# Perceiver kernel: the last share of x added on TensorE, normalising on ScalarE, values by token tile, and context loops with more lag and halved accumulations

## The chip, the cores and the metric

The kernel runs on one core of a Trainium2 chip. The metric is the device time of one execution in microseconds. The kernel before took 1700.06 us (median of three runs, 1695.6 to 1703.4). The engines are called by the profile's names: PE (TensorE; PEld is its weight load), DVE (VectorE), ACT (ScalarE), POOL (GpSimd) and SP (SyncE, which here issues most loads).

## What is computed

Two layers of a perceiver, all in float32. x is 512 tokens by 512 features, the context 8192 by 512; there are 16 heads of 32. Each of six steps adds to x a function of its layer norm (without weights):

```python
x = x + L0_xattn(_layernorm(x), ctx, ...)        # 512 queries against the keys the mask leaves
x = x + L0_attn(_layernorm(x), ...)              # self attention, keys j >= i
x = x + L0_ffn(_layernorm(x), ...)               # 8 experts, top 2, x * sigmoid(x)
x = x + L1_xattn(_layernorm(x), ctx, ctx, ...)   # cross attention with another mask
x = x + L1_attn(_layernorm(x), ...)              # self attention in a window of 64
x = x + L1_ffn(_layernorm(x), ...)               # 8 experts, top 2, relu squared
```

In the first cross attention the queries and keys are normalised per head, with weights. Of the context's 64 tiles of 128 keys the masks leave few; the kernel lists the tiles that have a key left and works on 15 such tiles ("slots"). A slower path for longer lists is in the program and isn't taken with these inputs.

## The kernel before

x stays in SBUF as four token tiles of 128 x 512. The 16 heads are worked on as four groups (g = 0 to 3) of four heads (h), so that one group fills 128 partitions: four matmuls with 32 rows or 32 columns of the array each. Scores are held keys by queries, 128 x 512 for one head and one slot. The softmax's maximum of each query is found first (`maxima`), and is then taken off the scores inside PSUM by a small bf16 matmul (`subtract`, L644) of three rows, the maximum split in three bf16 parts (`shift`), so that ACT's exp needs only the key's mask as its bias.

**Order.** Every engine works through its own queue in program order, and waits on semaphores that the framework places from the tiles' use. A tile pool hands out buffers; `bufs` is how many of one tag there are, and a tile waits until the earlier one in its buffer is read out. A pool that is opened in space that a closed pool left waits for that pool.

**Stages**, with their place in the profiled span: the list of context tiles (0 to 20 us), layer norm and queries (to 79), keys of layer 0's cross attention with the maxima of group 0 (to 201), its attention loop (to 476), outputs and layer norm (to 493), self attention 0 (to 641), router (to 672), experts (to 930), end and a branch for overfull experts (to 948), keys of layer 1's cross attention (to 1110), its attention loop (to 1353), outputs and layer norm (to 1372), self attention 1 (to 1480), router (to 1505), experts (to 1677), end (to 1698.5).

**The keys' loop** (`attend_slots`, first half). For slot s: `keys(s)` projects on PE into `pk` and adds a bias on DVE into `kb` (two buffers, L1055); `settle(s - 1)` transposes the unit keys of the slot before (`ktp`, L1064); `maxima(0, s - 2)` computes scores of group 0 and takes the maximum on DVE (L770); then perhaps one `values`; then `unit(s)`, the normalisation of `kb` on ACT and DVE (L1105, L1109). In layer 0 ACT also scans layer 1's mask (L1210) in this stage. In layer 1 `settle` is empty.

**The attention loop** (L876 and on), 60 turns (four groups, 15 slots). A turn computes scores of group g, slot i, and in the first 41 turns also those for the maxima of 19 turns later. It does so in two batches (j = 0, 1) of two heads each: two `sc`, two `scm` (three buffers), two subtractions, two exp on ACT (L874), two maxima on DVE (L770). After the batch j = 0 comes `accumulate` (L829): the four matmuls of the turn before, exp(scores) times values, 512 columns each, into one PSUM bank `acc`. POOL sums the exponentials of four slots (`add_up`, L847), and `denominators` (L856) sums those over the keys on PE with a matrix of ones into `den`, which has one of the four buffers of the scores ("s"). `divide` (L866, DVE) makes the reciprocals from PSUM in halves, and POOL multiplies. Such extra steps ("fillers": the transposes `mtp` and `stp` of the next shift, `denominators`, `divide`, `outputs`, and in layer 0 six steps that list layer 1's tiles) are queued with the turn in which they are due, one in a turn. In the last turns, without maxima, all four heads go in one batch.

**Outputs** (L717, L720): the group's normalised result times Wo on PE into `ops`, which DVE adds to x, group by group. The last group is finished in halves (`finish_part`: copy on ACT L697, reciprocal L687, product L688, bias L691 on DVE).

**Layer norm** (L187 to L198), per token tile: bn_stats and bn_aggr on DVE, square root on ACT, reciprocal and normalising on DVE (`xn`, L194), four transposes on PE (`lnt`, L197), copy on ACT (L198).

**Self attentions** follow an order written out by hand, a string for `in_order`: q and k are projections (`prj`, L1258), V the values of one token tile, M maxima, S shift, W weighted sums, F finish, O outputs, E and T the last group's parts. Their weights are loaded on SP's queue when the stage's pool opens.

**The FFN's end** (L1879 to L1886): DVE adds the rows gathered for each token (`got` times its gate) to x; a last matmul (`xps`, L1883) adds the rows of the tail, and DVE adds that to x. A branch on overfull experts (L1889 to L1892) follows, whose body isn't executed here.

Of the kernel before, what the change touches and what calls it, by code (L numbers as in the profile page):

```python
# [57 lines left out]
def tile_perceiver(  # L58
# [6 lines left out]

    const = ctx.enter_context(tc.tile_pool(name="const", bufs=1))
# [9 lines left out]
    dram = ctx.enter_context(tc.tile_pool(name="dram", bufs=1, space=bass.MemoryType.DRAM))  # L76
# [22 lines left out]
    with tc.tile_pool(name="begins", bufs=1) as tmp, tc.tile_pool(name="beginsps", bufs=1, space=PSUM) as tps:  # L99
# [60 lines left out]

    def bcast(pool, name, n):

        t = pool.tile([P, n], F32, name=f"bc_{name}", tag=f"bc_{name}", bufs=1)
        nc.sync.dma_start(out=t, in_=a[name].partition_broadcast(P))
        return t
# [16 lines left out]
    def layernorm_t(pool, psum, tag, xnT, off, order=range(NT), after=None):  # L182

        xn = pool.tile([P, NT, D], F32, name="xn", tag="xn", bufs=1)
        for t in order:
            st = small.tile([P, 6], F32, name="ln_s", tag="ln_s")
            nc.vector.bn_stats(st, x[:, t, :])  # L187
# [6 lines left out]
            nc.vector.tensor_scalar(xn[:, t, :], x[:, t, :], mv[:, 0:1], r, ALU.subtract, ALU.mult)  # L194
# [3 lines left out]
            nc.scalar.copy(xnT[:, :, off + t * P : off + (t + 1) * P], tp)  # L198
            if after is not None:
                after(t, xn)  # L200
        return xn

# [219 lines left out]
    def cross_attention0():  # L422
        with ExitStack() as st:
            pool = st.enter_context(tc.tile_pool(name="c0", bufs=2))
            ctxp = st.enter_context(tc.tile_pool(name="ctxp0", bufs=2))
            psum = st.enter_context(tc.tile_pool(name="c0ps", bufs=2, space=PSUM))
            pacc = st.enter_context(tc.tile_pool(name="c0acc", bufs=1, space=PSUM))
# [3 lines left out]
            with tc.tile_pool(name="c0q", bufs=2) as qp:  # L431
# [8 lines left out]
            kvp = st.enter_context(tc.tile_pool(name="c0kv", bufs=NCHUNK // 2))  # L440
# [70 lines left out]
    def cross_attention1():  # L511
        with ExitStack() as st:
            pool = st.enter_context(tc.tile_pool(name="c1", bufs=2))
            ctxp = st.enter_context(tc.tile_pool(name="ctxp1", bufs=2))
            psum = st.enter_context(tc.tile_pool(name="c1ps", bufs=2, space=PSUM))
            pacc = st.enter_context(tc.tile_pool(name="c1acc", bufs=1, space=PSUM))
# [3 lines left out]
            with tc.tile_pool(name="c1q", bufs=2) as qp:  # L520
# [7 lines left out]
            kvp = st.enter_context(tc.tile_pool(name="c1kv", bufs=NCHUNK))  # L528
            mp = st.enter_context(tc.tile_pool(name="c1m", bufs=2))
# [38 lines left out]
    def tile_list(tmp, psum, counts, bad, tag, out):  # L568
# [8 lines left out]
        nc.tensor.transpose(tp, counts, ident)  # L577
        nc.vector.tensor_copy(rows, tp)
# [4 lines left out]
        nc.tensor.matmul(ps, lhsT=tri, rhs=some, start=True, stop=True)  # L583
        place = tmp.tile([n, 1], F32, name="place", tag="place")
# [7 lines left out]
        nc.tensor.matmul(ps[:, SLOTS : SLOTS + 1], lhsT=ones[0:n, 0:1], rhs=some, start=True, stop=True)  # L592
        row = tmp.tile([1, SLOTS + 1], F32, name="row", tag="row")
# [10 lines left out]
        ps = psum.tile([P, SLOTS], F32, name="kbp", tag=tag)  # L604
        nc.tensor.matmul(ps, lhsT=rows, rhs=taken, start=True, stop=True)
        kbias = small.tile([P, SLOTS], F32, name="kbias", tag="kbias")
        nc.vector.tensor_scalar(kbias, ps, 1.0, BIG, ALU.subtract, ALU.mult)
# [22 lines left out]
    def in_quads(pool, psum, pacc, qT, wo, bv, late, splits=None):  # L630
# [55 lines left out]
        def divided(g, r, d, den):  # L686
            nc.vector.reciprocal(d[:, r], den)  # L687
            nc.vector.tensor_tensor(k.o[g][:, r], k.o[g][:, r], d[:, r], ALU.mult)  # L688
            if bv is not None:

                nc.vector.tensor_scalar(k.o[g][:, r], k.o[g][:, r], bv[:, g : g + 1], None, ALU.add)  # L691
# [21 lines left out]
        def outputs(g, tiles):  # L713

            for t in tiles:
                ps = tile_s(name="ops")
                nc.tensor.matmul(  # L717
                    ps, lhsT=k.o[g][:, t * P : (t + 1) * P], rhs=wo()[:, g, :], start=True, stop=True
                )
                nc.vector.tensor_tensor(x[:, t, :], x[:, t, :], ps, ALU.add)  # L720
# [1435 lines left out]
```

## Time and profile before

The profiled execution took 1700.19 us, its span is 1698.5 us; 1.7 us lie around the span. TensorE's granted clock is 0.938 of full on average.

| stage, us | PE busy | DVE busy | ACT busy | POOL busy | granted clock |
|---|---|---|---|---|---|
| 20 to 79, queries | 50.98 of 59 | 31.18 | 17.18 | 15.81 | 0.94 |
| 79 to 201, keys of layer 0 | 109.81 of 122 | 73.53 | 70.50 | 8.50 | 0.96 |
| 201 to 476, attention loop 0 | 268.89 of 275 | 182.08 | 153.70 | 164.92 | 0.96 |
| 476 to 493, outputs, layer norm | 7.86 of 17 | 12.72 | 3.12 | 1.48 | 0.84 |
| 493 to 641, self attention 0 | 137.91 of 148 | 71.99 | 38.34 | 16.29 | 0.91 |
| 672 to 930, experts 0 | 254.95 of 258 | 37.20 | 38.33 | 19.08 | 0.99 |
| 1110 to 1353, attention loop 1 | 239.55 of 243 | 155.19 | 147.12 | 163.82 | 0.99 |
| 1353 to 1372, outputs, layer norm | 10.59 of 19 | 12.81 | 3.44 | 0.96 | 0.72 |
| 1372 to 1480, self attention 1 | 94.14 of 108 | 62.44 | 25.00 | 6.65 | 0.94 |
| 1677 to 1698.5, end | 8.13 of 21.5 | 8.22 | 0.82 | 0.00 | 0.58 |

A row is one stretch of the span, with the busy time of each engine in it and the share of the full clock that PE was granted. A busy PE may still be slow: a matmul that lasts longer at a lower clock, or whose neighbour waits for a buffer, counts as busy. In the profile's other lines `out<-in` are the names of tiles, `128*32` the weights and `128x512` the moving operand of a matmul, and `[2.87 <-DVE o L691]` the idle time ahead of an instruction and what ended it. One float32 matmul makes two records, so an accumulation of four matmuls shows as x8.

### The profile page before, as it was taken

What the parts mean: (1) busy time and instruction counts of PE and PEld (TensorE: products, weight loads), DVE (VectorE), ACT (ScalarE), POOL (GpSimd) and SP (SyncE); (2) the same over time, 40 slices, a digit from 0 to 9 for tenths busy, and PEclk for the clock granted to TensorE, in tenths of its full rate; (3) what the DMA queues carried; (4) which work ended last, traced back from release to release, by engine and by line L of the source; (5) the groups of instructions that cost most, each with busy time, mean ns of one, the idle gap of its engine ahead of it and who ended that gap; (6) DMA issues with size and microseconds to landing.
All of it is one profiled execution on the core that took longest, in us unless ns stands there. A gap on an engine that the chain in (4) does not pass through costs nothing. (4 is left out here: it accounts for less than half of the span.)

```text
span 1698.5 us, 24206 instructions
## 1 busy us (share of the span) xinstructions
PE 1559.3 (92%) x9877; PEld 908.3 (53%) x9877; DVE 775.3 (46%) x1394; ACT 570.7 (34%) x1081; POOL 446.5 (26%) x345
## 2 busy tenths in 40 slices
PE   5888999999979996999999799999999989779996
PEld 2333333333234446999998456433333245369995
DVE  5466677774633655111112133667765526831112
ACT  1356355556622231111111211155556612211110
POOL 6000057787110011000002100078786010010002
PEclk9999989999989977999999899899999989879996
DMA  7145200000030004877784400000000040066572
GB/s 249 50 136 180 74 1 1 1 1 1 1 131 1 1 1 177 326 257 267 284 293 155 156 26 19 25 1 1 1 1 1 1 152 11 25 237 216 187 246 92
DMA packets 83928, 169.32 MB, mean 100 GB/s; under 512 B 5106, under 2 KB 20498, under 8 KB 82384
## 3 DMA queue, kind: packets, MB, share of 16 engines
q1 hardware_dynamic: 77200, 147.87, 25.4%
q0 software_dynamic: 6016, 17.55, 3.0%
q10 hardware_dynamic: 576, 2.10, 0.4%
q8 instruction: 84, 1.38, 0.3%
q14 instruction: 52, 0.43, 0.1%
HBM read 156.82 MB, written 9.63 MB: 98 GB/s over the span
## 5 line engine op out<-in xcount | busy, mean ns | idle before, releaser
L874 ACT ACTIVATE pT<-sc,kbias 128x512 f32<-128x512 f32 x480 | 299.4, 687 | 205.3 <-PE sc L644 142.8
L757 PE MATMUL sc<-qTf,kTf 32*128 32x512 f32 x1264 | 299.4, 660 | 6.1 <-DVE d L866 4.9
L770 DVE SCALAR_TENSOR_TENSOR mx<-scm,kbias,mx 128x512 f32<-128x512 f32 x312 | 215.4, 743 | 98.2 <-PE scm L757 95.8
L757 PE MATMUL scm<-qTf,kTf 32*128 32x512 f32 x656 | 241.2, 654 | 2.1 <-DVE mx L770 2.1
L1801 PE MATMUL y<-hT,w 128*128 128x112 f32 (+13 forms) x1536 | 211.0, 297 | 0.6 <-DVE hT L1976 0.6
L1785 PE MATMUL hps<-tokens,w 128*128 128x112 f32 (+13 forms) x1536 | 208.5, 295 | 0.0
L1801 PEld LDWEIGHTS y<-hT,w 128*128 128x128 f32 x1536 | 204.3, 197 | 2.5 <-DVE hT L1976 0.8
L1785 PEld LDWEIGHTS hps<-tokens,w 128*128 128x128 f32 x1536 | 201.5, 195 | 1.7
L847 POOL TENSOR_TENSOR four<-four,pT 128x2048 f32<-128x2048 f32 x42 | 190.7, 4540 | 9.7 <-ACT pT L874 6.7
L757 PEld LDWEIGHTS sc<-qTf,kTf 32*128 32x128 f32 x1264 | 91.3, 190 | 147.8 <-issue 111.5
L847 POOL TENSOR_TENSOR four<-pT 128x2048 f32<-128x2048 f32 x24 | 109.0, 4544 | 109.2 <-ACT pT L874 109.2
L829 PE MATMUL acc<-pT,vNf 128*32 128x512 f32 x960 | 133.7, 623 | 1.5 <-ACT o L836 1.5
L770 DVE SCALAR_TENSOR_TENSOR mx<-sc,kbias,mx 128x512 f32<-128x512 f32 x136 | 93.3, 744 | 80.3 <-PE sc L757 80.3
L1976 DVE TENSOR_TENSOR hT<-sg,hps 128x264 f32<-128x264 f32 (+7 forms) x64 | 28.0, 437 | 189.5 <-ACT sg L1975 189.5
L644 PE MATMUL sc<-shift,ones 3*128 3x512 bf16 (+3 forms) x544 | 100.1, 383 | 3.6 <-DVE shift L679 3.6
L757 PEld LDWEIGHTS scm<-qTf,kTf 32*128 32x128 f32 x656 | 75.0, 188 | 49.8 <-DVE mx L770 38.0
L1826 POOL DMA_DIRECT2D answers_d<-yb x17 | 9.5, 559 | 311.5 <-ACT yb L1819 311.4
L1975 ACT ACTIVATE sg<-hps 128x264 f32<-128x264 f32 (+7 forms) x64 | 25.4, 397 | 137.4 <-PE hps L1785 137.4
L829 PEld LDWEIGHTS acc<-pT,vNf 128*32 128x32 f32 x960 | 20.7, 109 | 88.0 <-issue 80.6
L658 DVE TENSOR_REDUCE neg<-mtp 128x4 f32<-128x512 f32 x64 | 41.2, 683 | 53.8 <-PE mtp L655 53.8
L1981 DVE TENSOR_TENSOR hT<-sg 128x224 f32<-128x224 f32 (+7 forms) x32 | 14.7, 459 | 107.6 <-ACT sg L1980 107.6
L1016 PE MATMUL pv<-wkvf,cslot 128*128 128x512 f32 x120 | 59.1, 639 | 0.2 <-ACT vNf L1025 0.2
(340 smaller groups left out, 1833.8 us busy)
## 6 DMA issues: line engine op xcount, KB each, us to landing
w<-in_L_ffn_W SPq DMA_DIRECT2D x96, 1024.0 KB, 7.4
mi<-in_mask SPq DMA_DIRECT2D x32, 512.0 KB, 4.2
cslot<-in_ctxT SPq DMA_DIRECT2D x30, 256.0 KB, 4.9
answers_d<-yb POOLq DMA_DIRECT2D x15, 256.0 KB, 7.1
answers_d<-zero POOLq DMA_DIRECT2D x9, 256.0 KB, 6.6
wkvf<-in_L_xattn_WkvT ACTq DMA_DIRECT2D x4, 512.0 KB, 6.5
wq<-in_L_xattn_WqT SPq DMA_DIRECT2D x2, 1024.0 KB, 7.5
wof<-in_L_xattn_WoT SPq DMA_DIRECT2D x2, 1024.0 KB, 4.7
```

What stands on the lines that cost most here:

```text
L644: nc.tensor.matmul(ps, lhsT=ones16[r, :], rhs=k.shifts[g][r, 0:w], start=start, stop=stop)
L658: nc.vector.tensor_reduce(neg[:, h, :], tp.rearrange("p (t k) -> p t k", k=P), AX.X, ALU.max, negate=True)
L757: nc.tensor.matmul(ps, lhsT=kT[HD * h : HD * (h + 1), g, i * P : (i + 1) * P], rhs=qT[HD * h : HD * (h + 1), g, :], start=True, stop=stop,)
L770: nc.vector.scalar_tensor_tensor(to, ps, b, to, ALU.add, ALU.max)
L829: nc.tensor.matmul(k.sums[g][HD * h : HD * (h + 1), :], lhsT=vN[:, i, g * P + HD * h : g * P + HD * (h + 1)], rhs=pT[:, h, :], start=(i == ...
L847: engine.tensor_tensor(to, parts[g][-1], pT, ALU.add)
L874: nc.scalar.activation(pT[:, h, :], ps, AF.Exp, bias=kbias[:, i : i + 1])
L1016: last = nc.tensor.matmul(ps.rearrange("p (g n) -> p g n", g=NG), lhsT=src[:, c, s % 2, :], rhs=wkv[:, :, c, i * P : (i + 1) * P], start=( ...
L1785: nc.tensor.matmul(ps[:, j, 0:k], lhsT=w1[:, c, f * P : (f + 1) * P], rhs=tokens[:, c, starts[r] : starts[r] + k], start=(c == 0), stop=(c ...
L1801: nc.tensor.matmul(accs[0][:, d, 0:k], lhsT=w2[:, f, d * P : (d + 1) * P], rhs=hT[:, f, 0:k], start=(c == 0 and f == 0 and d % 2 == 0), st ...
L1975: nc.scalar.activation(sg, ps, AF.Sigmoid)
L1976: nc.vector.tensor_tensor(dst, sg, ps, ALU.mult)
```

## The change

1. Nearly all pools are opened with `reuse_waits="tile"`: the first tile in a new pool waits only for the old tiles that lay in the same place, not for the whole old pool.
2. Keys' loop: `settle` lags by two slots and `maxima` by three, with three buffers of `kb`.
3. Attention loop: an accumulation is done in two halves of 256 columns, one after each batch, for the turn before; in the turns without maxima it is whole and lags by two. pT has five buffers rather than four. `den` is copied to SBUF by ACT for the first three groups, and the reciprocals read the copy.
4. The listing of layer 1's tiles goes in nine steps rather than six, with a pause between a PE result and its use.
5. For the last group, PE first puts x into the bank (identity times x) and adds the outputs to it; DVE takes the statistics of the next layer norm from PSUM and ACT copies the sum to x (`x_from`). The FFN's end does so too; in layer 1 only the copies, alternately on ACT and DVE. Inside the branch the statistics would be taken again.
6. Layer norm: normalising is one ACT instruction (scale r, bias -mean r; the bias is a small DVE instruction), and the transposed tiles are copied by DVE and ACT in turn. In the self attentions the bias of `o` moves from DVE to ACT.
7. The values of the self attentions are projected inside the layer norm, after each token tile's transposes, and V leaves the order strings; `wv` is loaded first.

```diff
+    def tile_pool(**kw):
+
+        return tc.tile_pool(reuse_waits="tile", **kw)
...
-            nc.vector.tensor_scalar(xn[:, t, :], x[:, t, :], mv[:, 0:1], r, ALU.subtract, ALU.mult)
+            back = small.tile([P, 1], F32, name="ln_b", tag="ln_b")
+            nc.vector.tensor_scalar(back, mv[:, 0:1], r, -1.0, ALU.mult, ALU.mult)
+            nc.scalar.activation(xn[:, t, :], x[:, t, :], AF.Identity, scale=r, bias=back)
...
-            nc.scalar.copy(xnT[:, :, off + t * P : off + (t + 1) * P], tp)
+            if t % 2:
+                nc.scalar.copy(xnT[:, :, off + t * P : off + (t + 1) * P], tp)
+            else:
+                nc.vector.tensor_copy(xnT[:, :, off + t * P : off + (t + 1) * P], tp)
...
+    def x_from(t, ps):
+
+        st = small.tile([P, 6], F32, name=f"ln_s{t}", tag=f"ln_s{t}", bufs=1)
+        nc.vector.bn_stats(st, ps)
+        nc.scalar.copy(x[:, t, :], ps)
+        stats[t] = st
...
-                nc.vector.tensor_scalar(k.o[g][:, r], k.o[g][:, r], bv[:, g : g + 1], None, ALU.add)
+                nc.scalar.activation(k.o[g][:, r], k.o[g][:, r], AF.Identity, bias=bv[:, g : g + 1])
...
-            for t in tiles:
-                ps = tile_s(name="ops")
+            both = [(t, tile_s(name="ops")) for t in tiles]
+            if g == NG - 1:
+                for t, ps in both:
+                    nc.tensor.matmul(ps, lhsT=ident, rhs=x[:, t, :], start=True, stop=False)
+            for t, ps in both:
                 nc.tensor.matmul(
-                    ps, lhsT=k.o[g][:, t * P : (t + 1) * P], rhs=wo()[:, g, :], start=True, stop=True
+                    ps, lhsT=k.o[g][:, t * P : (t + 1) * P], rhs=wo()[:, g, :], start=(g < NG - 1), stop=True
                 )
-                nc.vector.tensor_tensor(x[:, t, :], x[:, t, :], ps, ALU.add)
+                if g == NG - 1:
+                    x_from(t, ps)
+                else:
+                    nc.vector.tensor_tensor(x[:, t, :], x[:, t, :], ps, ALU.add)
...
-            if s >= 1:
-                settle(s - 1)
             if s >= 2:
-                maxima(0, s - 2)
+                settle(s - 2)
+            if s >= 3:
+                maxima(0, s - 3)
...
-        def accumulate():
-
-            if last is None:
+        def accumulate(lag, halves=(0, 1)):
+
+            if len(behind) < lag:
                 return
-            g, i, pT = last
-            if i == 0:
+            g, i, pT = behind[0]
+            r = slice(halves[0] * S // 2, (halves[-1] + 1) * S // 2)
+            if i == 0 and halves[0] == 0:
                 k.sums[g] = pacc.tile([P, S], F32, name="acc", tag="acc")
             for h in range(GH):
                 nc.tensor.matmul(
-                    k.sums[g][HD * h : HD * (h + 1), :],
+                    k.sums[g][HD * h : HD * (h + 1), r],
                     lhsT=vN[:, i, g * P + HD * h : g * P + HD * (h + 1)],
-                    rhs=pT[:, h, :], start=(i == 0), stop=(i == n - 1),
+                    rhs=pT[:, h, r], start=(i == 0 and halves[0] == 0), stop=(i == n - 1 and halves[-1] == 1),
                 )
+            if halves[-1] == 0:
+                return
+            behind.pop(0)
...
+            if g < NG - 1:
+                d = late().tile([P, S], F32, name="d", tag="d", bufs=1)
+                nc.scalar.copy(d, dens[g])
+                dens[g] = d
...
-            pT = late().tile([P, GH, S], F32, name="pT", tag="pT", bufs=4)
+            pT = late().tile([P, GH, S], F32, name="pT", tag="pT", bufs=5)
...
-                    if j == 0:
-                        accumulate()
+                    accumulate(1, (j,))
...
-                accumulate()
+                accumulate(2)
...
-                kb = kvp.tile([P, D], F32, name="kb", tag="kb")
+                kb = kvp.tile([P, D], F32, name="kb", tag="kb", bufs=3)
...
-                more, EARLY, aside, scanned, [listing] * 6,
+                more, EARLY, aside, scanned, [listing] * 9,
...
+            wv = load(pool, a["L0_attn_wv"], [P, NG, NC, P], "wv")
             wq = load(pool, a["L0_attn_wq"], [P, NC, D], "wq")
...
+            layernorm_t(pool, psum, "s", xnT, 0, after=lambda t, xn: value(t))
+            add_bias(bo)
...
-                "q0 k0 q1 M0.0 k1 M0.1 V0 M0.2 V1 M0.3 V2 S0.0 S0.1 M1.0 V3 M1.1 S0.2 q2 W0.0 M1.2 W0.1 M1.3 k2 "
+                "q0 k0 q1 M0.0 k1 M0.1 M0.2 M0.3 q2 S0.0 S0.1 M1.0 k2 M1.1 S0.2 W0.0 M1.2 W0.1 M1.3 "
...
-                "q0 k0 V0 M0 V1 V2 q1 S0.0 V3 S0.1 V4 k1 M1 S0.2 q2 S1.0 W0 k2 S1.1 M2 F0 S1.2 q3 S2.0 W1 k3 S2.1 "
+                "q0 k0 M0 q1 S0.0 k1 S0.1 M1 q2 S0.2 S1.0 W0 k2 S1.1 M2 F0 S1.2 q3 S2.0 W1 k3 S2.1 "
...
-                ps = psum.tile([P, D], F32, name="xps", tag="m")
+                ps = psum.tile([P, D], F32, name="xps", tag="h", bufs=4)
+                nc.tensor.matmul(ps, lhsT=ident, rhs=x[:, t, :], start=True, stop=False)
                 nc.tensor.matmul(
-                    ps, lhsT=gb[0:tail, t * P : (t + 1) * P], rhs=yb[0:tail, :], start=True, stop=True
+                    ps, lhsT=gb[0:tail, t * P : (t + 1) * P], rhs=yb[0:tail, :], start=False, stop=True
                 )
-                nc.vector.tensor_tensor(x[:, t, :], x[:, t, :], ps, ALU.add)
+                if layer == 0:
+                    x_from(t, ps)
+                else:
+                    (nc.scalar.copy if t % 2 else nc.vector.tensor_copy)(x[:, t, :], ps)
```

## The prediction

> **What bounds the kernel now.** I read, in this order: the share of each engine, the list of what TensorE (PE) waited for, the timeline of PE and of its weight loads through one turn of the attention loop, and the timelines of the hand-overs between stages. TensorE is busy 1559.3 of 1698.5 us, so at most 139 us of its idling can go; the rest must come from matmuls that are stretched by a buffer wait or by a half clock, which count as busy.
>
> ```profile
> PE 1559.3 (92%) x9877; PEld 908.3 (53%) x9877; DVE 775.3 (46%) x1394; ACT 570.7 (34%) x1081; POOL 446.5 (26%) x345
> ```
>
> The waits of PE (total us, times, longest). The four shown are those that the change touches; they make 51 us.
>
> ```profile
> PE lnt L197 <- DVE xn L194: 23.9, 8, 9.9
> PE ktp L1064 <- DVE kb L1109: 12.0, 7, 3.1
> ...
> PE ops L717 <- DVE o L691: 10.1, 5, 2.9
> ...
> PE sc L757 <- DVE d L866: 4.9, 6, 1.8
> ```
>
> One ordinary turn of the attention loop, PE's timeline. Two batches of scores (`sc` of this turn, `scm` for the maxima of a later one), each followed by the subtraction L644, and the accumulation L829 once.
>
> ```profile
> 291.35 0.70 PE L757 MATMUL sc<-qTf,kTf 32*128 32x512 f32 x2
> ...
> 292.31 0.38 PE L644 MATMUL sc<-shift,ones 3*128 3x512 bf16 x2
> 292.33 0.59 PE L757 MATMUL sc<-qTf,kTf 32*128 32x512 f32 x2
> ...
> 292.96 1.10 PE L757 MATMUL scm<-qTf,kTf 32*128 32x512 f32 x2
> ...
> 293.91 0.59 PE L757 MATMUL scm<-qTf,kTf 32*128 32x512 f32 x1
> 294.43 1.07 PE L829 MATMUL acc<-pT,vNf 128*32 128x512 f32 x8
> ```
>
> The first batch takes 0.96 us (291.35 to 292.31), the second 2.10 (292.33 to 294.43), though it is the same work: it starts right behind the first and finds the three `scm` buffers not yet taken by VectorE. The weight loads say so: `[0.65 <-DVE mx L770]`. Then 1.00 for the accumulation; the turn is 4.07 (291.35 to 295.42).
>
> **The loop: accumulation in halves.** After the change each batch is followed by half an accumulation, so the second batch starts later and the buffer wait lies under the first half. Cost of a half: the nearest row is the self attention's 256-column accumulation, 551.04, whose eight records are over when `den` begins at 551.50.
>
> ```profile
> 551.04 0.64 PE L1344 MATMUL acc<-pT,vNs 128*32 128x256 f32 x8
> 551.50 0.61 PE L1344 MATMUL den<-pT,ones 128*32 128x256 f32 x8
> ```
>
> That is 0.46, or 0.55 where another shape follows (`den` here, to the `mtp` at 552.05). A turn becomes 2 x (0.96 scores + 0.31 subtraction + 0.55) = 3.64. [...] The row (0.46 against 0.88, a ratio of 0.52) is the same operand kinds on this chip, so I take the row. A turn that holds the outputs as a filler supports 3.64: it lasts 5.46, of which 1.92 are the outputs, leaving 3.54 where the wait is covered. Gain per ordinary turn: 4.07 - 3.66 = 0.41.
>
> The starts of the L829 groups give the turns. Layer 0: 18 ordinary turns, x 0.41 = 7.4; six with `mtp` or `stp`, which hide part of the wait already, half of it: 1.2; two turns after `den` of 5.40 and 5.47, which wait for the reciprocal to free a PSUM buffer: with `den` first copied to SBUF by ScalarE (0.59 in the row of `d<-den`) they come down to about 4.07, 2.7. The last `den`: turns of 6.32 and 4.31 where neighbours take 2.3 to 2.4.
>
> ```profile
> 433.33 1.13 PE L757 MATMUL sc<-qTf,kTf 32*128 32x512 f32 x6
> 436.25 1.19 PE L757 MATMUL sc<-qTf,kTf 32*128 32x512 f32 x1 [1.79 <-DVE d L866]
> ...
> 438.65 1.94 PE L829 MATMUL acc<-pT,vNf 128*32 128x512 f32 x8
> ```
>
> The idle is 1.79, but everything behind it runs at half speed until 442.96 (an accumulation of 1.94 instead of 1.06). [...] by the rows 5.8. The rows decide; I take 4.5, since the copy itself still stands between. Listing of layer 1's tiles, five turns of 4.38 to 8.26, together 27.7 against 5 x 4.07 = 20.4: spread over nine, three steps fewer wait for their own result: 5 of the 7.3. Layer 0's loop: 7.4 + 1.2 + 2.7 + 4.5 + 5 = **-21**. Layer 1's loop, no listing: 27 ordinary turns 11, seven with fillers 1.4, after `den` 2.9, last `den` 3.5 (turns of 5.17 and 3.92): 18.8; I take **-17**, as its engines have the least slack.
> What is late next: GpSimd adds eleven times 4.54 in fifteen turns, 3.33 a turn, VectorE takes four times 0.68 = 2.73 plus the fillers, ScalarE two pairs of 1.27 = 2.54. All under 3.66, GpSimd by a tenth only. The new lag of one and the fifth pT buffer keep an accumulation from waiting for its own exponentials.
>
> **Keys of layer 0, 79 to 201 us.** The transposes wait for the unit keys, 12.0 in seven waits, and `pk` for its addition 1.7. Behind the longest the clock halves: `pv` x8 took 5.33 at 91.61 where 3.60 is usual at 96.78. One slot more of lag with a third `kb` removes these waits. Per slot PE has 6.85 of work, VectorE 5.3, ScalarE 5.5, so PE stays the bound, but ScalarE's scan of the mask is in the same queue. Between -16 (with the clock) and -4 (waits move to the single `pk`): **-9**. Layer 1's settle is empty: 0.
>
> **Self attention's head.** Before: end of the last `den`, ops, layer norm, first projection.
>
> ```profile
> 479.00 1.98 PE L717 MATMUL ops<-wof,o 128*128 128x512 f32 x4 [2.87 <-DVE o L691]
> 482.40 1.98 PE L717 MATMUL ops<-wof,o 128*128 128x512 f32 x4 [1.42 <-DVE o L691]
> 487.28 1.79 PE L197 MATMUL lnt<-ident,xn 128*128 128x128 f32 x8 [2.90 <-DVE xn L194]
> 490.63 1.97 PE L197 MATMUL lnt<-ident,xn 128*128 128x128 f32 x8 [1.56 <-DVE xn L194]
> 493.27 5.02 PE L1258 MATMUL prj<-xnT,wq 128*128 128x512 f32 x6 [0.67 <-ACT xnT L198]
> ```
>
> The four ident x matmuls added (0.86 each, 3.4) lie in the 2.87 for `o` and push ops by 0.5. VectorE loses four additions of 0.68, two biases of 0.35 and four normalisations of 0.53: 5.5; ScalarE gets the copies of x (0.59 each), the bias and the normalisation (0.76 by the row of `kTf`, which also has scale and bias by pointer), and its 1.28 table load, which ran at 475.22, now lies behind the copies. The values' matmuls enter between the transposes, the first at about 487.2, 6.1 earlier than `prj`. Their weights: the loads were held by the whole old pool until 484.52; now `wv` goes first and waits only for the last scores, near 470, so it is there. But the values no longer fill gaps further on: M0.1 to M0.3 then wait for VectorE (2.3) and W0.0 for its shift and exponentials (1.4), and the transposes stretch by 0.9. Layer 0 net **-1.5** (between -5 and +2). Layer 1: 19.0 from `den` to `prj`, with ops at half clock (2.78 and 3.78); first values 7.5 earlier, 1.5 given back: **-6** (-9 to -2).
>
> **Other joints.** First layer norm (20 to 79): 0, +-1, the keys' weights bound it. End of self attention 0 into FFN 0: four ident matmuls 2.6 in a busy stretch against waits of 1.1 and 1.7 shortened: -0.5. Self attention 1 into the router: the idle of 3.64 at 1481.04 and 0.84 and 1.15 before it: **-3.5**. FFN 0's end: ident x stands ahead of the selected rows and waits for VectorE's additions, +1.5, against 1.7 saved after the branch where the statistics are ready: 0. The statistics inside the branch aren't executed. FFN 1's end loses:
>
> ```profile
> 1664.07 12.95 PE L1801 MATMUL y<-hT,w 128*128 128x48 f32 x64
> 1677.35 1.10 PE L1817 MATMUL stp<-ident,answers 128*112 128x128 f32 x4 [0.33 <-ACT answers L1810]
> 1679.17 7.00 PE L1883 MATMUL xps<-yb,gb 112*128 112x512 f32 x8 [0.72 <-ACT yb L1819]
> ```
>
> Eight records, four matmuls, take 7.00 at half clock, 1.75 each. Eight matmuls would take 14.0. They start only when x0 has its gathered rows, 1680.9, and end by 1695 against 1686.2; if the clock comes back midway, by 1691. Copies at the end cost as the additions did. **+4.5** (+3 to +9).
> Elsewhere the pools' finer waits only let loads start earlier under work that doesn't wait for them: 0.
>
> **Sum**, against the profiled execution's own 1700.2 (span 1698.5 and 1.7 around; the median of the runs, 1700.06, is the same): -9 -21 -17 -1.5 -6 -0.5 -3.5 +4.5 = -54, **1646 us**.
>
> **Rivals.**
> *Half of the loop's gain stays out.* GpSimd's adds need 3.33 to 3.5 a turn and hold pT; each den step then waits for it, and the keys only move their wait to `pk`. For: GpSimd is at 164.9 of 275 us in layer 0's loop, all of it in three quarters of it. Against: even shortened by 16, those 207 us hold 164. Half of 38 and of 9 stays out: 1646 + 23 = 1669. Chance 0.25.
> *More comes.* [...] the keys give 16, the heads 9 and 5: 1630. Chance 0.13.
> *Slower: [...].* The place is L829 in the 82 turns with two batches (41 in each layer). [...] a turn takes 2 x (0.96 + 0.31 + 1.1) = 4.74 and the loops lose 82 x 0.67 = 55 where the forecast wins 21 (7.4, 1.2, 11 and 1.4): with the other gains of 33 left, 1722. It decides from a half of about 0.97 us upward, where 82 turns have lost 33 (0.76 for the loop alone). Against it the row of 0.46. Chance 0.06.
> *The halves gain nothing and the rest half:* about 1697, within 0.5%: chance 0.04.
> The likeliest, 1638 to 1657, has 0.52. From these, faster by over 0.5% (8.5 us, about what a measurement of this kernel can tell from no change) 0.90, within 0.5% 0.04, slower 0.06. The range 1624 to 1682 leaves out the last two and the edge of the others.
>
> **What would show it.** Ordinary turns of 3.6 to 3.7 between successive L829 pairs and no `scm` weight load waiting on `mx`; turns behind `den` without a wait for L866's line; the row `ktp <- kb` nearly gone; the first `vNs` matmul before 488; FFN 1's end longer by some us after the last `y`. Wrong would be: halves above 0.75 us, waits on pT for GpSimd, `pk` waiting on `kb`, or the values waiting for ScalarE's normalisation.

## The result and the profile after

The changed kernel takes 1691.43 us (median of 20 runs, 1685.11 to 1703.41) against 1701.07 before (20 runs); the ratio is 0.9952 with a 95% interval of 0.9936 to 0.9968. That is faster by half a percent, where 1646 was forecast. The profiled execution took 1685.11 us, its span is 1683.3; it is the fastest of the twenty, so its trace shows 15.2 of gain where the medians show 9.6 (why is told under the clock below). Ratios here and below leave out runs in a slow state, of which there was one (2564.6 us, among e1's 22).

First the page's line of engine shares, then four of PE's waits (total us, times, longest), after the change.

```profile
PE 1551.2 (92%) x10565; PEld 925.3 (55%) x10565; DVE 767.9 (46%) x1373; ACT 601.5 (36%) x1132; POOL 449.7 (27%) x345
```

```profile
PE lnt L207 <- ACT xn L204: 17.2, 8, 7.2
...
PE scm L786 <- DVE mx L799: 10.2, 5, 3.0
...
PE ops L743 <- POOL o L908: 6.3, 2, 3.2
...
PE pk L1053 <- DVE kb L1092: 4.9, 4, 1.4
```

The waits of the transposes for the unit keys (12.0) and of the scores for the reciprocal (4.9) have left the list, and so has `ops` for the bias (10.1). Three others stand in their places: `scm` for the maxima, `ops` for GpSimd's product, `pk` for the addition. PE still is the bound.

The same stretches of both profiled executions, each between two marks on PE's timeline:

| stretch | before | after | change | forecast |
|---|---|---|---|---|
| start to last `qtp` | 74.0 | 75.7 | +1.7 | 0 |
| keys of layer 0, to the first `stp` | 136.4 | 129.1 | -7.3 | -9 |
| loop of layer 0, to the end of the last `den` or `acc` | 265.8 | 258.2 | -7.6 | -21 |
| hand-over and self attention 0, to `lps` | 169.2 | 170.0 | +0.8 | -2 |
| both routers, `lps` to `gps` | 32.5 | 36.4 | +3.9 | 0 |
| FFN 0 and its end, to the first `pk` | 302.4 | 304.6 | +2.2 | 0 |
| keys of layer 1, to `stp` | 133.5 | 134.6 | +1.1 | 0 |
| loop of layer 1 | 258.0 | 251.0 | -7.0 | -17 |
| hand-over and self attention 1, to `lps` | 129.0 | 122.5 | -6.5 | -9.5 |
| FFN 1, end | 197.8 | 201.1 | +3.3 | +4.5 |

The loops miss 23 us of their 38, the joints that were put at nothing cost 9. Not all of the 9 is the change's: the first stretch takes between 72 and 76 in the traces of the fourteen versions, in no order, and the first router's +2.1 is the clock's (below).

**The halves are as cheap as the row said.** PE's timeline of a half turn after the change (a turn is two of these; the lines of `scm` between are left out):

```profile
276.57 0.70 PE L786 MATMUL sc<-qTf,kTf 32*128 32x512 f32 x2
...
277.53 0.38 PE L667 MATMUL sc<-shift,ones 3*128 3x512 bf16 x2
277.84 0.64 PE L861 MATMUL acc<-pT,vNf 128*32 128x256 f32 x8
278.41 0.70 PE L786 MATMUL sc<-qTf,kTf 32*128 32x512 f32 x2
```

From 276.57 to 278.41 are 1.84, a turn is 3.69 (before 4.07); the half itself takes 0.57 (277.84 to 278.41). The forecast had 0.55. Its 0.88 for a whole accumulation, beside which it put the 0.46, is one amid others in the trace before, from 470.77 to 471.65:

```profile
470.77 1.06 PE L829 MATMUL acc<-pT,vNf 128*32 128x512 f32 x8
471.65 1.04 PE L856 MATMUL den<-four,ones 128*32 128x512 f32 x8
```

In the ordinary turn before a whole one took 0.99 (294.43 to 295.42).

**Behind `den` the wait moved.** The reciprocals in VectorE's timeline before, layer 0, and then ScalarE, VectorE and PE after:

```profile
300.40 3.37 DVE L866 RECIPROCAL d<-den 128x256 f32<-128x256 f32 x2 [2.35 <-PE den L856]
303.69 4.18 DVE L770 SCALAR_TENSOR_TENSOR mx<-scm,kbias,mx 128x512 f32<-128x512 f32 x6
```

```profile
291.28 0.59 ACT L897 COPY d<-den 128x512 f32<-128x512 f32 x1 [2.75 <-PE den L891]
...
291.90 3.36 DVE L903 RECIPROCAL d<-d 128x256 f32<-128x256 f32 x2 [3.41 <-ACT d L897]
...
295.18 2.63 DVE L799 SCALAR_TENSOR_TENSOR mx<-scm,kbias,mx 128x512 f32<-128x512 f32 x4
...
295.88 0.69 PE L786 MATMUL scm<-qTf,kTf 32*128 32x512 f32 x1 [1.76 <-DVE mx L799]
```

The copy frees the PSUM bank, but in both kernels VectorE has both reciprocals, one right behind the other, ahead of this turn's maxima. The maxima start 3.36 later, and `scm`, with three buffers, waits for them. The copy itself (0.59) now stands in front of the reciprocals. The turn takes 6.36 (4.52 and 1.84); before it took 5.40, and in e2 below, which has the halves without the copy, 5.75.

**Group 2's outputs came due too early.** Layer 0, after, POOL and PE in the turns without maxima:

```profile
424.63 3.13 POOL L906 TENSOR_TENSOR o<-o,d 128x512 f32<-128x512 f32 x1 [7.97 <-DVE d L903]
...
427.28 1.07 PE L861 MATMUL acc<-pT,vNf 128*32 128x512 f32 x8
...
427.85 3.60 POOL L908 TENSOR_SCALAR o<-o,bvC 128x512 f32<-128x512 f32 x1
...
431.50 3.63 PE L743 MATMUL ops<-wof,o 128*128 128x512 f32 x4 [3.16 <-POOL o L908]
```

The turns of 6.32 and 4.31, behind the last `den`, did fall to 2.28, as forecast. But fillers are due by turn number, and GpSimd's product and bias take the time they take (3.13 and 3.60 here; before they took 3.12 and 1.56, and in the 3.60 VectorE adds exponentials): `ops` waits 3.16 and then runs at half speed, 3.63 instead of 1.98. The two turns of the outputs take 13.3 where they took 8.9.

### The profile page after: what moved, and what is told of

The parts are those of the page before. It is cut to its first block, busy times and chain, and to the rows that moved or that the text cites. A ratio compares the mean times of both kernels' runs of the same rounds, so it can differ in the third digit from the quotient of the medians.

```text
span 1683.3 us, 25532 instructions
## 1 busy us (share of the span) xinstructions
PE 1551.2 (92%) x10565; PEld 925.3 (55%) x10565; DVE 767.9 (46%) x1373; ACT 601.5 (36%) x1132; POOL 449.7 (27%) x345
## 5 line engine op out<-in xcount | busy, mean ns | idle before, releaser
L799 DVE SCALAR_TENSOR_TENSOR mx<-scm,kbias,mx 128x512 f32<-128x512 f32 x312 | 219.3, 745 | 72.4 <-PE scm L786 69.9
L786 PE MATMUL scm<-qTf,kTf 32*128 32x512 f32 x656 | 224.4, 670 | 10.2 <-DVE mx L799 10.2
L786 PEld LDWEIGHTS sc<-qTf,kTf 32*128 32x128 f32 x1264 | 83.8, 187 | 121.0 <-issue 78.1
L861 PE MATMUL acc<-pT,vNf 128*32 128x256 f32 (+1 forms) x1600 | 146.5, 438 | 1.6 <-ACT o L871 1.6
L861 PEld LDWEIGHTS acc<-pT,vNf 128*32 128x32 f32 x1600 | 32.1, 108 | 133.5 <-issue 127.7
L667 PE MATMUL sc<-shift,ones 3*128 3x512 bf16 (+3 forms) x544 | 95.0, 377 | 3.6 <-DVE shift L702 3.6
L2028 DVE TENSOR_TENSOR hT<-sg 128x224 f32<-128x224 f32 (+7 forms) x32 | 14.7, 459 | 107.7 <-ACT sg L2027 107.7
```

Of the source, the lines that this page charges most:

```text
L667: nc.tensor.matmul(ps, lhsT=ones16[r, :], rhs=k.shifts[g][r, 0:w], start=start, stop=stop)
L786: nc.tensor.matmul(ps, lhsT=kT[HD * h : HD * (h + 1), g, i * P : (i + 1) * P], rhs=qT[HD * h : HD * (h + 1), g, :], start=True, stop=stop,)
L799: nc.vector.scalar_tensor_tensor(to, ps, b, to, ALU.add, ALU.max)
L861: nc.tensor.matmul(k.sums[g][HD * h : HD * (h + 1), r], lhsT=vN[:, i, g * P + HD * h : g * P + HD * (h + 1)], rhs=pT[:, h, r], start=(i == ...
```

## The experiments

Ratios are to the kernel before, timed beside each run, since its own time differs from chip to chip (1699.5 to 1707.8); so runs are to be compared by their ratios (0.001 is 1.7 us), and medians only roughly. "e6" below is the fastest that the first four gave, so later parts were undone on it.

| run | ratio | 95% interval | median us |
|---|---|---|---|
| after | 0.9952 | 0.9936 to 0.9968 | 1691.4 |
| e1 whole accumulations | 0.9979 | 0.9965 to 0.9994 | 1699.1 |
| e2 before + halves | 0.9981 | 0.9965 to 0.9997 | 1702.1 |
| e4 outputs later | 0.9854 | 0.9828 to 0.9879 | 1680.4 |
| e5 listing | 0.9866 | 0.9839 to 0.9893 | 1679.7 |
| e6 quarters, outputs later | 0.9770 | 0.9746 to 0.9794 | 1662.1 |
| e7 end of FFN 1 | 0.9926 | 0.9900 to 0.9951 | 1688.1 |
| f1 = e6, values in the strings | 0.9810 | 0.9779 to 0.9841 | 1671.3 |
| f2 = e6, normalising on VectorE | 0.9740 | 0.9709 to 0.9771 | 1659.4 |
| f3 = e6, plain pools | 0.9821 | 0.9787 to 0.9855 | 1674.1 |
| f4 = e6, FFN ends as before | 0.9731 | 0.9697 to 0.9765 | 1657.1 |
| h1 = e6, attention outputs as before | 0.9761 | 0.9737 to 0.9786 | 1666.7 |
| g1 all that helped | 0.9641 | 0.9609 to 0.9673 | 1643.3 |

**e1, whole accumulations.**

```diff
-                    accumulate(1, (j,))
+                    if j == 0:
+                        accumulate(1)
```

> The changed kernel (median 1691.4) with the accumulation whole again after the batch j = 0, all else as changed. Theory A (the halves gain what was forecast in ordinary turns, 4.07 to 3.69, but the turns with fillers give part of it back): ordinary turns return to 4.07, 45 of them x 0.38 = 17 us lost, the turns behind den fall from 6.4 to about 5.4 and the listing's worst turn shrinks, 8 to 10 us won back: about 1699. Theory B (waits that go are paid back by a lower granted clock, whatever the loop does): within 3 us of 1691.

Measured 0.9979, as theory A had it, though the turns behind `den` in layer 0 take 6.8 and 5.9 and not its 5.4. Its loops take 266.8 and 258.6 us, those of before 265.8 and 258.0: without the halves the other loop edits earn nothing. The nine steps of the listing are among them: from the first `stp` to the next `mtp` it takes 60.4, before 60.3.

**e2, the halves alone on the kernel before** (the loop over `halves` as in the change, lag one, five pT buffers).

> The kernel before with the halved accumulations alone (and five pT buffers). Theory A: ordinary turns 4.07 to 3.69, 45 of them, 17 us; the turns with mtp, ops and den keep their length, those behind den and the listing's get longer and ops waits for GpSimd, together 5 to 8 given back: 1700 less 10, about 1690. Rival (the forecast's step, that all turns with two batches gain and nothing is given back): 1680 or less.

Measured 0.9981, a gain of 3 us where theory A had 10. Its profiled execution (1708.4) lies high among its own. There the ordinary turns are 3.69 too, but the stretch with the listing takes 3.9 more than before, and the turns behind the second `den` take 8.1 and 4.6 with a half clock; the loops take 266.1 and 256.2. Neither the halves nor the rest of the loop's edits gains much by itself; together they take 7 us off each loop.

**e6, reciprocals in quarters behind their turn's maxima, outputs three turns later.**

```diff
-            r = slice(i * S // 2, (i + 1) * S // 2)
-            nc.vector.reciprocal(dens[g][:, r], dens[g][:, r])
+            r = slice(i * S // 4, (i + 1) * S // 4)
+            with tc.issue_after(taken[-1].ins):
+                nc.vector.reciprocal(dens[g][:, r], dens[g][:, r])
...
-                    (at + 7, lambda g=g: k.outputs(g, (0, 1))),
-                    (at + 8, lambda g=g: k.outputs(g, (2, 3))),
+                    (at + 6, lambda g=g: divide(g, 2)),
+                    (at + 7, lambda g=g: divide(g, 3)),
+                    (at + 10, lambda g=g: k.outputs(g, (0, 1))),
+                    (at + 11, lambda g=g: k.outputs(g, (2, 3))),
```

> The changed kernel with den's reciprocal in four pieces, each queued behind the maxima of its own turn, and the outputs of groups 0 to 2 due three turns later. Theory A: scm's waits of 1.8 to 2 us behind the 3.36 us of reciprocals go (four turn pairs, about 1.5 to 2 us each), and the wait of ops for GpSimd's o (3.16 us, twice) with the half clock behind it (about 1.7 each) goes: 6 to 8 plus 9 to 10, that is about 1676. Theory B (given back by the clock): above 1687.

Measured 1662.1, 29 below the changed kernel (31 by the ratios), twice what was expected; the two traces differ by 20.6. The same places in its timelines, layer 0:

```profile
292.06 1.41 DVE L800 SCALAR_TENSOR_TENSOR mx<-scm,kbias,mx 128x512 f32<-128x512 f32 x2 [3.90 <-PE scm L787]
...
295.23 0.94 DVE L905 RECIPROCAL d<-d 128x128 f32<-128x128 f32 x1
...
296.09 1.31 DVE L800 SCALAR_TENSOR_TENSOR mx<-scm,kbias,mx 128x512 f32<-128x512 f32 x2
```

```profile
429.20 1.07 PE L862 MATMUL acc<-pT,vNf 128*32 128x512 f32 x8
430.20 1.98 PE L743 MATMUL ops<-wof,o 128*128 128x512 f32 x4
432.11 1.14 PE L787 MATMUL sc<-qTf,kTf 32*128 32x512 f32 x8
```

The maxima start with their turn, a quarter (0.94) fits between them, and `ops` starts without a wait at 1.98. The loops take 249.6 and 241.2: 16.2 and 16.9 less than before. The listing's loss is still in the first.

**e4, outputs two turns later alone.**

```diff
-                    (at + 7, lambda g=g: k.outputs(g, (0, 1))),
-                    (at + 8, lambda g=g: k.outputs(g, (2, 3))),
+                    (at + 9, lambda g=g: k.outputs(g, (0, 1))),
+                    (at + 10, lambda g=g: k.outputs(g, (2, 3))),
```

> The changed kernel with the outputs of groups 0 to 2 due two turns later and the reciprocals as changed. Theory A: the wait of ops for GpSimd's o and the half clock behind it go, 8 us in each layer as in the profile of the version with both: 1675, the rest to 1662 belongs to the reciprocals and to the spread that their half clock brings. Rival: the later outputs alone only move the wait, and the reciprocals carried it: 1685 or more.

Measured 1680.4, between the two: layer 1's loop is 246.0, 5.0 less than after, and e6 takes another 4.8 off it (layer 0's is 254.5, 3.8 less). The two waits are worth about the same in the trace, and by the ratios too: the later outputs take 0.0098 off (17 us), the quarters 0.0084 more (14 us).

**Why more in the medians than in the trace: the clock.** e7 has the changed kernel's loop untouched. PE behind the second `den` of layer 0, in e7 and then after the change:

```profile
360.85 1.21 PE L786 MATMUL scm<-qTf,kTf 32*128 32x512 f32 x1 [1.83 <-DVE mx L799]
...
361.86 1.06 PE L786 MATMUL scm<-qTf,kTf 32*128 32x512 f32 x1
362.85 1.08 PE L861 MATMUL acc<-pT,vNf 128*32 128x256 f32 x8
```

```profile
363.93 0.69 PE L786 MATMUL scm<-qTf,kTf 32*128 32x512 f32 x1 [1.83 <-DVE mx L799]
...
364.46 0.59 PE L786 MATMUL scm<-qTf,kTf 32*128 32x512 f32 x1
364.98 0.64 PE L861 MATMUL acc<-pT,vNf 128*32 128x256 f32 x8
```

The same code and the same wait of 1.83 us; in one execution the matmuls behind it take 1.06 and the accumulation 1.08, in the other 0.59 and 0.64. What differs in the two traces is where the wait lies. In each trace of this case all changes of the granted clock (40 to 54 in a trace; 45 before, 43 after) lie on one grid of 3.41 us, and the grid begins elsewhere in each execution (the cells below begin at 357.12 in e7 and at 359.76 after, 2.64 apart). The cells of this grid around the two waits, in e7 and then after (each line: the stretch, its length, busy time of PE, PEld, DVE, ACT and POOL, the granted clock, and the DMA's share and GB/s):

```profile
357.12:360.53 3.41, 1.90 (x20) 0.46 (x14) 3.41 (x3) 1.27 (x2) 2.02 (x2) 1.00 0.01 2
360.53:363.94 3.41, 3.09 (x16) 0.77 (x16) 2.33 (x4) 0.95 (x2) 2.68 (x2) 0.50 0.02 5
363.94:367.35 3.41, 3.41 (x22) 0.84 (x22) 1.29 (x2) 1.21 (x3) 3.01 (x1) 0.50 0.00 0
```

```profile
359.76:363.17 3.41, 2.34 (x24) 0.46 (x14) 3.23 (x2) 1.35 (x3) 2.29 (x1) 1.00 0.01 2
363.17:366.58 3.41, 2.65 (x22) 0.86 (x22) 2.68 (x5) 1.27 (x2) 2.93 (x3) 1.00 0.03 5
```

In e7 1.51 of the 1.83 fall into one cell, and the next two cells have half the clock. After the change the wait is cut into 1.07 and 0.76, and the clock stays. The traces of after, e4, e5 and e7 hold sixteen such waits behind a reciprocal (1.76 to 1.84): behind six of them, with 1.26 to 1.83 in one cell, the clock fell for one or two cells; behind ten, with 0.93 to 1.27, it stayed. This is no rule for every loop: in e1 and before the clock fell behind waits with as little as 0.81 and 1.10 in one cell, and what else counts there is open. The stretch between two groups' `mtp` that holds the wait took 68.8 in e7 and e4, 65.8 in the profiled execution after, and 63.3 in e6 and each of the versions made from it. So a wait of this length costs itself, and by chance 1.6 or about 3 us more. All four waits of the profiled execution after kept the clock; e7 lost it behind three, which cost 6.2: 3.0 behind the one shown (68.8 against 65.8), 3.2 behind the other two. That is the size of the 6 us between the changed kernel's profiled execution and its median; that it is their cause is argued, since only one of its twenty executions has a trace. Other things spread the times too: g1 has no such waits, and its six runs lie within 14 us.

**e5, the listing.** VectorE's steps on one element read an operand from PSUM (`row` isn't copied first), and the maximum of the counts comes after the second loop.

```diff
-        nc.vector.tensor_copy(row, ps)
...
-            nc.vector.tensor_tensor(none, none, bad, ALU.add)
+            nc.vector.scalar_tensor_tensor(none, ps[:, SLOTS : SLOTS + 1], 0.0, bad, ALU.is_equal, ALU.add)
...
-        nc.vector.tensor_tensor(row[:, SLOTS : SLOTS + 1], row[:, SLOTS : SLOTS + 1], none, ALU.add)
+        end = nc.vector.tensor_tensor(irow[:, SLOTS : SLOTS + 1], ps[:, SLOTS : SLOTS + 1], none, ALU.add)
```

> The changed kernel with the listing's last steps rewritten so that VectorE's two-operand instructions on one element read one operand from PSUM, and the maximum of both layers' counts taken later. Theory A: the 4.35 us of the one-element addition is VectorE held back by GpSimd's 4.54 us addition when both operands lie in SBUF; it becomes about 0.15, scm no longer waits 2.99 and the half clock behind it goes: turns of 6.69 and 3.45 become about 2.2 and 1.85, 5 to 6 us faster, 1686. Rival: the addition waits for something else (its operand `bad`), then it stays long and the time stays at 1691.

Measured 1679.7, a larger gain than theory A's 1686. The step in VectorE's and GpSimd's timelines, first before, then after the change, then in e5:

```profile
249.78 3.55 DVE L601 TENSOR_TENSOR row<-row,none 1x1 f32<-1x1 f32 x1
...
248.81 4.52 POOL L847 TENSOR_TENSOR four<-four,pT 128x2048 f32<-128x2048 f32 x1 [3.33 <-ACT pT L874]
```

```profile
249.28 0.14 DVE L622 TENSOR_SCALAR none<-row 1x1 f32<-1x1 f32 x1
249.46 4.35 DVE L624 TENSOR_TENSOR none<-none,bad 1x1 f32<-1x1 f32 x1
...
249.29 4.50 POOL L882 TENSOR_TENSOR four<-pT 128x2048 f32<-128x2048 f32 x1 [2.33 <-ACT pT L911]
```

```profile
247.12 0.14 DVE L627 TENSOR_TENSOR irow<-row,none 1x1 int32<-1x1 f32 x1
...
246.97 4.53 POOL L881 TENSOR_TENSOR four<-pT 128x2048 f32<-128x2048 f32 x1 [2.33 <-ACT pT L910]
```

After the change the addition of one element, begun 0.17 behind GpSimd's, ends with it at 253.8, and `scm` waits 2.99 for the maxima queued behind it. In e5 the last addition, with an operand in PSUM (`row` is the PSUM tile there), takes 0.14 though it begins 0.15 behind GpSimd's. The stretch from the first `stp` to the next `mtp` is 53.2 instead of 58.3, 5.1 less. The medians differ by 11.7, but the profiled executions only by 3.9: the one after lies 6.3 below its median and e5's 1.5 above.

**e7, the end of FFN 1 as before.**

```diff
+                if layer == 0:
                     nc.tensor.matmul(ps, lhsT=ident, rhs=x[:, t, :], start=True, stop=False)
...
-                    (nc.scalar.copy if t % 2 else nc.vector.tensor_copy)(x[:, t, :], ps)
+                    nc.vector.tensor_tensor(x[:, t, :], x[:, t, :], ps, ALU.add)
```

> The changed kernel with the end of layer 1's FFN as before: no identity matmuls, VectorE adds the last rows to x. Theory A: the end gets the 3.0 us back that the profile shows it lost after the last expert (xps start to end of span), 1688. Theory B: no change that can be told from 1691.

Measured 1688.1, the 3 us (4 by the ratio), though the interval overlaps that of the changed kernel. In the trace the stretch of FFN 1 is 197.6 again (after 201.1, before 197.8).

**f1 to f4 and h1, one part undone on e6.** f1 puts `V` back in the strings as they were before; f2 restores the line of L194 and copies on ScalarE; f3 opens the pools without `reuse_waits="tile"`; f4 restores L1883 to L1886 in both layers; h1 restores `outputs` (L712 to L720).

> The version with the reciprocal in quarters and later outputs (1662.1, the steadiest so far) with the values of the self attentions back in the order strings. Theory C (from the profile: values by token tile gave about 4 us in layer 1 and cost about 2 in layer 0, since there they no longer fill the waits for maxima): 1664. Rival, the forecast's own step (gains of 1.5 and 6): 1669.

0.9810 against e6's 0.9770, about 7 us, though the intervals overlap. The stretches to `lps` grow by 3.6 and 5.7 us without the values by token tile. The 5.7 is clear: versions with the same code there lie between 121.2 and 122.5 in layer 1. In layer 0 they lie between 169.4 and 175.5 (e4), so neither the 3.6 nor theory C's loss of 2 can be told. The forecast's 7.5 was for these hand-overs as a whole.

> The same version with the layer norm's normalising back on VectorE and all transposed copies on ScalarE. Theory D: ScalarE's chain of table load, copies of x and normalising (0.8 us each instead of 0.53) is what made both routers 1.9 us longer than before, so they come back and the heads stay: 1658. Rival: VectorE, with the statistics, is the later one and the heads get longer: 1665 or more.

0.9740, not clear of e6. The trace shows both signs: self attention 0 gets 2.4 longer with VectorE (within the spread just told), self attention 1 3.4 shorter, the second router 3.7 shorter (15.8), the stretch from `xps` to the next keys 4.3 shorter. The theory is right for three hand-overs of five; the first router stays (17.3). Part of the second router's 3.7 is lost again: the experts behind it and the end take 204.4 in this trace, 200.9 to 203.0 in the versions with the same code there.

> The same version with plain pools, whose first tile waits for the whole pool that lay there. Theory E: the values' weights then are issued only after the last outputs' reads, some 9 us before they land, so the first values start late in both self attentions, 3 us or more each, and the keys' loop is untouched: 1668 or more. Rival: something else covers the loads: 1662.

0.9821; the intervals just overlap. The trace shows 3.5 in self attention 1 and nothing clear in self attention 0 (1.1), and the values there don't wait for their weights (issued at 459.12, the first values at 464.14). So the theory's size holds for one of two; the pools' finer waits seem to help, by 3 us in the trace and 9 by the ratios, and how is open.

> The same version with the FFN's end of both layers as before (no identity matmuls, VectorE adds the last rows, the next layer norm takes its own statistics). Theory A: layer 1 gives 3 back, and layer 0, where the stretch from xps to the next keys grew from 32.0 to about 35 to 37 us, 3 to 4: 1656. Rival: only layer 1's 3: 1659.

0.9731, about the expected 1656, though the interval overlaps e6's. The stretch behind FFN 0 is 30.1 instead of 36.5, the end of FFN 1 2.9 shorter: x through PE costs more than the addition did here.

> The version with quarters and later outputs (1662.1) with the attentions' last outputs as before: no identity matmuls, VectorE adds to x, and each next layer norm takes its own statistics (the FFN's ends stay as changed). Theory A (the forecast's step: VectorE loses four additions in each of four hand-overs while the identity matmuls lie in a wait): 1.5 to 2 us more in each, 1669. Rival (the copies of x on ScalarE and the identity matmuls cost what the additions cost): 1660 to 1664.

0.9761 against 0.9770: no difference that can be told. The stretches to `lps` are 3.1 and 5.2 longer, the routers 1.4 and 1.9 shorter. Clear of the spread and of the clock's moments is layer 1 alone: there the last share of x on PE takes 5.2 off the hand-over and gives 1.9 back in the router.

**g1, all that helped**: e6, e5, f4, and normalising on ScalarE in self attention 0 alone.

> All that helped: reciprocals in quarters with later outputs (1662), the listing's rewritten steps (11 less on the changed kernel, of which its profile shows 5 to 8), both FFN ends as before (5 less), normalising on ScalarE in layer 0's self attention only and on VectorE elsewhere (3 to 5 less). Theory A: 1645, if the parts add up. Rival: the FFN end's and the normalising's gains are the same one, 1650.

0.9641 (0.9609 to 0.9673), 3.6% below before and 3.1% below the changed kernel. Its loops take 242.4 and 241.1, together 40.3 less than before.

## Why the prediction was wrong

**What held.** The cost of a half (0.55 forecast, 0.57 measured) and so the ordinary turn (3.66, measured 3.69); the keys (-9, measured -7.3, waits of 12.0 gone and 3.2 more on `pk`); the end of FFN 1 (+4.5, measured +3.3; the first `xps` waits 2.50 for x, and the clock comes back midway); self attention 1 in part (-9.5, measured -6.5). PE stayed the bound, and no wait on pT for GpSimd's adds shows in PE's list.

**The step that failed: the loops' sum, -38, measured -14.6.** Its terms in layer 0:

- Ordinary turns, -7.4: 18 x 0.38 = 6.8. Right.
- Six turns with `mtp` or `stp`, "half of it", -1.2: measured -0.9. The four with `mtp` got nothing, 4.73 before, 2.87 + 1.84 = 4.71 after: the filler had lain in the buffer wait (it adds 0.66 to an ordinary turn before, 1.02 after). The two with `stp` got all of it, 4.38 and 4.73 before, 4.02 and 4.30 after. The outputs' turns, to which no term was given, went from 5.46 to 5.60.
- Behind `den`, "they come down to about 4.07", -2.7: 6.36 and 6.44 instead of 5.40 and 5.47, +1.9. The step looked at the PSUM bank only; the reciprocals' 3.36 on VectorE, with the maxima queued behind, was the next wait, and the copy came in front of it. That an engine would be late was a rival for GpSimd and not for VectorE, whose 2.73 a turn leave 0.9 in a turn of 3.64: room for a quarter of the reciprocal (0.94), not for two halves of 1.7.
- The last `den`, -4.5: the two turns fell by 6.1, more than forecast, and the outputs' two turns grew by 4.4, since `ops` was due before GpSimd was done. "What is late next" was asked for the ordinary turn and not for the filler some turns on.
- The listing, -5: nothing (e1: 60.4 against 60.3). Its worst turn waits not for its own results, which the longer schedule spaces, but for one VectorE instruction on a single element that stands 4.35 us while GpSimd adds. Before it was the same (L601, 3.55 beside an addition of 4.52); the forecast had the turn of 8.26 and had not opened it.

Layer 1 has no listing and repeats the third and fourth: +1.8 behind `den`, -4.5 in the two turns behind the last one, +4.4 in the outputs' turns.

With the third and fourth cause taken away the loops came to -16.2 and -16.9 (e6), with the listing's too to -23.4 and -16.9 (g1): the forecast's -38 was there to be had, behind waits that the change itself brings or leaves.

The time came out between two of the rivals, 1669 and 1697, and neither was what happened. "Half of the loop's gain stays out" put the loss on GpSimd's adds, which no PE wait shows. "Within 0.5%", at a chance of 0.04, took it that the halves gain nothing, and they gained what was forecast. The slower rival's 1.1 us for a half was supposed, with no row behind it; 0.57 was measured.

**What was put at nothing.** Behind FFN 0 (+3.5 from `xps` to the next keys) and in the second router (+1.8) normalising on ScalarE lies on the path: f2 takes 4.3 and 3.7 off them. The first of these is a rough figure, since the nine traces with the change's code there give 33.0 to 37.9 us; f2, f4 and g1 lie below all of them. The first router's +2.1 is the clock's and comes with either code:

```profile
645.30 1.95 PE L1697 MATMUL lps<-router,xnTf 128*128 128x8 f32 x16 [0.36 <-ACT xnTf L198]
```

```profile
633.09 3.58 PE L1738 MATMUL lps<-router,xnTf 128*128 128x8 f32 x16 [1.69 <-ACT xnTf L209]
```

Before (the first line) these sixteen records ran at full clock, after (the second) at half: the clock fell 2.6 us behind the first of them before and 0.3 us ahead of it after. e2, with the code of before in this place, has 3.58 and a router of 16.8; e5, with the changed code, has 1.95 and 14.7. Self attention 0 (+0.8 against -2) can't be judged from these traces: the changed code takes 169.4 to 175.5 there, the code of before 169.2 and, in e2, 172.7.

And a gain read from one trace is not the median's. The forecast priced the wait of 1.79 for the last reciprocal by its rows. In the trace before this wait (434.46 to 436.25) lies whole in one cell of the grid, and the granted clock was 0.50 in the two cells behind it, to 443.09. Of the change's own waits (after, e4, e5, e7) those with 1.26 to 1.83 us in one cell were followed by the half clock too, those with 0.93 to 1.27 not. The forecast did not ask what the new waits would do to the clock.

## What to carry to other kernels

When a wait is taken from a loop, look at every kind of turn that has something extra in it: a filler that lay in the old wait now costs its whole time, and a filler due by a count of turns comes earlier in time than the engine that feeds it. An engine's mean load a turn says little; ask what its longest instruction does to the one queued behind it. Give the piece a size that fits the slack (0.94 in place of 3.36) and queue it behind the turn's urgent work. Where waits of one or two microseconds come and go, one trace is not enough: here the clock fell behind six of sixteen waits of 1.76 to 1.84 us, and the same wait fell on either side in two executions.

## What was not expected of the hardware

A VectorE instruction on one element with both operands in SBUF stood 4.35 us (after, at 249.46) beside a GpSimd addition of 4.50 and ended with it; with one operand in PSUM (e5) it took 0.14 beside the same addition. The maxima, which read PSUM, kept their 0.75 beside a GpSimd addition (before, at 249.12). The clock changed on a grid of 3.41 us whose place differed from execution to execution, and the same wait of 1.83 us cost nothing more in one execution and 3 us more in another of the same code.
